# Seven products in place of eight for the down projection of a linear-attention and dense-experts kernel

## The chip, the cores and the metric

The kernel runs on one core of a Trainium2 chip. The metric is the device time of one execution in microseconds (us), as a median over runs. A core has engines with queues of their own: TensorE (PE in the profile; its weight loads are shown apart as PEld), VectorE (DVE), ScalarE (ACT), GpSimd (POOL) and SyncE (SP), which issues the DMAs here. Each engine works through its own instructions in the order in which the program issues them, and waits on semaphores for the others.

## The reference

Eight batches of 512 tokens with 128 channels, all in float32. First linear attention with a normalisation ahead, then a sum over eight experts.

```python
def _L0_attn_ref(x, gamma, beta, w_qkv, w_out, b_out):
    xn = (x - mean) / jnp.sqrt(var + EPS) * gamma + beta
    q, k, v = jnp.split(jnp.einsum('bnc,ck->bnk', xn, w_qkv), 3, axis=2)
    ...
    k = jax.nn.softmax(k, axis=1)
    context = jnp.einsum('bnhd,bnhe->bhde', k, v)
    out = jnp.einsum('bhde,bnhd->bnhe', context, q)
    ...
    return jnp.einsum('bnk,kc->bnc', out, w_out) + b_out + x

def _L0_ffn_ref(hidden_states, Wg, Wu, Wd):
    x = hidden_states.reshape(-1, H)
    def expert_step(acc, w):
        wg, wu, wd = w
        h = jax.nn.silu(x @ wg) * (x @ wu)
        return (acc + h @ wd, None)
    ...

x = x + _layernorm(_L0_attn_ref(_layernorm(x), ...))
x = x + _layernorm(_L0_ffn_ref(_layernorm(x), Wg, Wu, Wd))
```

Wg and Wu are 8 x 128 x 512, Wd is 8 x 512 x 128: with blocks of 128 there are 8 x 4 = 32 blocks of h for each token.

## The kernel before

**The main loop** (from line 564 on) runs over units: batches 0 and 7 are cut into two halves of 256 tokens each, batches 1 to 6 are whole, so there are ten units. For each unit it takes 32 steps (NSTEP: 8 experts times NF = 4 blocks of 128 hidden channels). A step i is:

- g = wg' zT (line 572) and u = wu' zT (574) on TensorE, each a product of a 128x128 block of weights with zT, the normalised batch with channels in partitions and 512 (or 256) tokens side by side, each into one of two PSUM buffers;
- sg = silu(g) on ScalarE (576), h = sg * u on VectorE (578);
- the down product of the step LAG = 2 earlier (line 532, function down): acc += wd' h, 32 such products in one PSUM bank;
- one turn of `others`, which is between(n): it gives every generator that is going one turn, in other words the work of one segment up to the next `yield`.

A float32 product shows as two records of the matmul and two of the weight load.

**Beside the steps** run two generators. attention(b + 1) makes the next batch's zT, and so counts its way in steps: pair_stats of x; the scaling to xh; the move to channels (to_channels); the activation to xnT; k, its maximum and its exponential; x1 and the bias; the move to tokens (to_tokens); the product g_ps, then c, m and wa, one step each; and after_wa, which forms y, normalises it, adds the residual (x2, on GpSimd), normalises again (z) and moves z to channels, which gives zT. finish(b) normalises the finished sum of the unit before, adds x2 on GpSimd and stores the result.

**Moves.** For batches 2 and later a change between tokens and channels in partitions goes in two parts: VectorE transposes blocks of 32x32 (lines 224 and 233), then carry() writes the tile to a DRAM buffer ("bounce", line 215) and reads it back in four DMAs (line 217), all on SP's queue. After it the generator yields LANDING = 4 times. Batches 0 and 1 transpose on TensorE in place of it.

**Normalisations.** norm_stats and pair_stats take statistics on VectorE and then one power on GpSimd (lines 172 and 194: rstd); norm_apply scales in four pieces on VectorE (line 200), which waits for that power.

**Order.** Nothing is reordered: what an engine does next is what the program issued next. In the loop a step issues g, u, sg, h, then the down product of an earlier step, then the segment of the generators. So the segment of step i stands on VectorE behind h of step i and ahead of h of step i + 1.

Of the kernel before, what the change touches and what calls it, by code (L numbers as in the profile page):

```python
# [1 line left out]

# [8 lines left out]
ALU = mybir.AluOpType  # L11
# [4 lines left out]
def kernel(  # L16
# [31 lines left out]


    nc = tc.nc  # L50
    B, N, C = x.shape
# [5 lines left out]
    NQ = P // Q  # L57
    LANDING = 4
    BY_TENSORE = (0, 1)
# [7 lines left out]
    xp = ctx.enter_context(tc.tile_pool(name="xp", bufs=3))  # L67
    work = ctx.enter_context(tc.tile_pool(name="work", bufs=2))
    small = ctx.enter_context(tc.tile_pool(name="small", bufs=3))
    hp = ctx.enter_context(tc.tile_pool(name="hp", bufs=4))  # L70
    dram = ctx.enter_context(tc.tile_pool(name="dram", bufs=4, space=bass.MemoryType.DRAM))
    blk = ctx.enter_context(tc.tile_pool(name="blk", bufs=2))
    ps_gu = ctx.enter_context(tc.tile_pool(name="ps_gu", bufs=2, space=bass.MemoryType.PSUM))
    ps_acc = ctx.enter_context(tc.tile_pool(name="ps_acc", bufs=1, space=bass.MemoryType.PSUM))
    ps = ctx.enter_context(tc.tile_pool(name="ps", bufs=3, space=bass.MemoryType.PSUM))

# [73 lines left out]
    def keep_warm(moving, count=1):  # L150

        t = ps_acc.tile([P, N], F32, tag="acc", name="unread")
        for i in range(count):
            nc.tensor.matmul(
                t[:, : moving.shape[1]], moving[:, :P], moving,
                start=(i == 0), stop=(i == count - 1),
            )


    def norm_stats(src, name):  # L160

        n = src.shape[1]
        stats = small.tile([P, n, 6], F32, tag=f"stats{n}", name=f"stats_{name}")
        mv = small.tile([P, n, 2], F32, tag=f"mv{n}", name=f"mv_{name}")
        for j in range(n):
            nc.vector.bn_stats(stats[:, j, :], src[:, j])
        for j in range(n):
            nc.vector.bn_aggr(mv[:, j, :], stats[:, j, :])  # L168
        ve = small.tile([P, n], F32, tag=f"ve{n}", name=f"ve_{name}")
        nc.vector.tensor_scalar_add(ve, mv[:, :, 1], EPS)  # L170
        rstd = small.tile([P, n], F32, tag=f"rstd{n}", name=f"rstd_{name}")
        nc.gpsimd.tensor_tensor(rstd, ve, mhalf[:, :n], ALU.pow)  # L172
        return mv, rstd
# [23 lines left out]
    def norm_apply(dst, src, mv_rstd):  # L197
        mv, rstd = mv_rstd
        for j in range(src.shape[1]):
            nc.vector.tensor_scalar(  # L200
                dst[:, j], src[:, j], mv[:, j, 0:1], rstd[:, j : j + 1],
                ALU.subtract, ALU.mult,
            )
# [32 lines left out]
    def by_block(t, n=NJ):  # L236

        return t.rearrange("c (j a i) -> c a j i", j=n, a=NQ)

    def flat(t):  # L240
        return t.rearrange("p j c -> p (j c)")
# [6 lines left out]
    def opening():  # L248
# [14 lines left out]
        ek = flat(work.tile([P, NQ, P], F32, tag="ek", name="ek_0"))  # L263
        v = const.tile([P, N], F32, name="v_0")
        qT = const.tile([P, N], F32, name="qT_0")
        x1 = work.tile([P, NJ, C], F32, tag="x1", name="x1_0")
        x1b = work.tile([P, NJ, C], F32, tag="x1b", name="x1b_0")
        x2 = xp.tile([P, NJ, C], F32, tag="x2", name="x2_0")
        x2s[0] = x2
        y = work.tile([P, NJ, C], F32, tag="y", name="y_0")  # L270
        yn = work.tile([P, NJ, C], F32, tag="yn", name="yn_0")
        z = work.tile([P, NJ, C], F32, tag="z", name="z_0")
        zT = work.tile([P, NQ, NJ, Q], F32, tag="zT", name="zT_0")
        kmax = small.tile([P, 3], F32, tag="kmax0", name="kmax_0")
# [101 lines left out]
    def attention(b):  # L376
        xt = xs[b]
        mv, r1, r2 = pair_stats(xt, f"1_{b}")
        yield
        xh = work.tile([P, NJ, C], F32, tag="xh", name=f"xh_{b}")  # L380
        norm_apply(xh, xt, (mv, r2))
# [6 lines left out]
        else:  # L388
            xhT = work.tile([P, NQ, P], F32, tag="xhT", name=f"xhT_{b}")
            to_channels(xh, xhT, f"xh_blk_{b}")  # L390
# [18 lines left out]
        nc.vector.reciprocal(rsum, ksum)  # L409
        x1b = work.tile([P, NJ, C], F32, tag="x1b", name=f"x1b_{b}")  # L410
        for j in range(NJ):
# [44 lines left out]
        y = work.tile([P, NJ, C], F32, tag="y", name=f"y_{b}")  # L456
        yn = work.tile([P, NJ, C], F32, tag="yn", name=f"yn_{b}")
        z = work.tile([P, NJ, C], F32, tag="z", name=f"z_{b}")
        zT = work.tile([P, NQ, NJ, Q], F32, tag="zT", name=f"zT_{b}")
        lags = [after_wa(b, lo, hi, xt, xnT, wa, x1b, x2, y, yn, z, zT) for lo, hi in WHOLE]  # L460
# [7 lines left out]
    def after_wa(b, lo, hi, xt, xnT, wa, x1b, x2, y, yn, z, zT):  # L468
# [11 lines left out]
        s3 = norm_stats(y[:, r], f"3_{b}_{lo}")  # L480
        yield
        norm_apply(yn[:, r], y[:, r], s3)
        (nc.gpsimd if b or lo else nc.vector).tensor_tensor(  # L483
# [4 lines left out]
        s4 = norm_stats(x2[:, r], f"4_{b}_{lo}")  # L488
        yield
        norm_apply(z[:, r], x2[:, r], s4)  # L490
        yield
# [9 lines left out]

    def finish(b, lo, hi, f):
        r = slice(lo, hi)
        n = hi - lo
        if n < NJ:
            f_ps = transpose4(f, f"f_ps_{b}_{lo}")
            f3 = f_ps.rearrange("p (j b k) -> p j b k", j=NJ, b=NQ)[:, :n]
        else:
            for _ in range(LANDING if b + 2 < B else 2 * LANDING):
                yield  # L510
            f3 = f.rearrange("p b (j k) -> p j b k", j=NJ)
        s5 = norm_stats(f3, f"5_{b}_{lo}")
        yield
        fn = work.tile([P, NJ, C], F32, tag="fn", name=f"fn_{b}_{lo}")
        norm_apply(fn[:, :n].rearrange("p j (b k) -> p j b k", b=NQ), f3, s5)
        o = work.tile([P, NJ, C], F32, tag="o", name=f"o_{b}_{lo}")
        nc.gpsimd.tensor_tensor(flat(o[:, :n]), flat(fn[:, :n]), flat(x2s[b][:, r]), ALU.add)  # L517
        nc.sync.dma_start(out[b].rearrange("(p j) c -> p j c", j=NJ)[:, r], o[:, :n])

    units = [(b, lo, hi) for b in range(B) for lo, hi in parts(b)]  # L520
    NSTEP = E * NF
    LAG = 2
    accs, fTs, hs = {}, {}, {}
    pending = []

    def down(n, i):
        b, lo, hi = units[n]
        if i == 0:
            accs[n] = ps_acc.tile([P, N], F32, tag="acc", name=f"acc_{n}")
        e, f = divmod(i, NF)  # L530
        cols = (hi - lo) * P
        nc.tensor.matmul(  # L532
            accs[n][:, :cols], wd_sb[e][:, f, :], hs.pop((n, i)),
            start=(i == 0), stop=(i == NSTEP - 1),
        )
        if i == NSTEP - 1:
            acc = accs.pop(n)[:, :cols].rearrange("c (a j i) -> c a j i", a=NQ, j=hi - lo)
            if hi - lo < NJ:
                fT = work.tile([P, N], F32, tag="fT", name=f"fT_{n}")
                nc.vector.tensor_copy(by_block(fT[:, :cols], hi - lo), acc)  # L540
                fTs[n] = fT[:, :cols]
            else:
                fTs[n] = work.tile([P, NQ, P], F32, tag="f", name=f"f_{n}")
                to_tokens(acc, fTs[n], f"f_blk_{n}")

    def between(n):

        b, lo, hi = units[n]
        if lo == 0 and b + 2 < B:
            xs[b + 2] = load_x(b + 2)  # L550
        going = rest[:]
        rest.clear()
        if n == 0:
            going.append(prepare())
        if hi == NJ and b + 1 < B:
            going.append(attention(b + 1))
        for i in range(NSTEP):
            if i == LAG + 1 and n > 0:
                going.append(finish(*units[n - 1], fTs.pop(n - 1)))
            going = [g for g in going if next(g, "end") != "end"]  # L560
            yield

    opening()
    for n, (b, lo, hi) in enumerate(units):
        zT = zTs.pop((b, lo))
        cols = (hi - lo) * P
        others = between(n)
        for i in range(NSTEP):
# [5 lines left out]
            nc.tensor.matmul(u_ps[:, :cols], wu_sb[e][:, w], zT, start=True, stop=True)  # L574
            sg = hp.tile([P, N], F32, tag="sg", name=f"sg_{n}_{i}")
            nc.scalar.activation(sg[:, :cols], g_ps[:, :cols], AF.Silu)  # L576
            h = hp.tile([P, N], F32, tag="h", name=f"h_{n}_{i}")
            nc.vector.tensor_tensor(h[:, :cols], sg[:, :cols], u_ps[:, :cols], ALU.mult)  # L578
            hs[n, i] = h[:, :cols]
            pending.append((n, i))  # L580
            if len(pending) > LAG:
                down(*pending.pop(0))
            next(others, None)
        for _ in others:
            pass
    while pending:
        down(*pending.pop(0))
    for _ in finish(*units[-1], fTs.pop(len(units) - 1)):
        pass
# [31 lines left out]
```

## Time and profile before

| | us |
|---|---|
| median of 3 runs (721.27 to 721.45) | 721.32 |
| the profiled execution | 721.76 |
| its span, first to last instruction | 719.8 |
| unit 0, first half of batch 0 | 41.8 |
| unit 1, second half of batch 0 | 49.6 |
| unit 2, batch 1 | 85.1 |
| units 3 to 7, batches 2 to 6, each | 85.7 |
| unit 8, first half of batch 7 | 42.5 |

A unit is counted from its first g to the next unit's first g. The rest of the span is the opening of 22.7 us (the attention of batch 0, with the first weights on their way) and the last unit with its end.

How to read the lines: a line of the timeline has the start and the length in us, the engine, the line of the kernel, the operation, what it writes and reads, its shape, how many instructions are merged in it, and in brackets the engine's idle time before it and what ended that. A line of the groups has the busy time of all its instructions, the mean of one in ns, and the idle time before them. Matmuls are pipelined: the time from one start to the next is what one costs, not the length of its record. PEclk is the clock granted to TensorE, as a share of full speed.

### The profile page before, as it was taken

To read this page: it belongs to the slowest core of one execution; us is meant where nothing else is said; L and a number is where in the kernel's file an instruction comes from. 1 tells how busy PE (TensorE), PEld (TensorE's weight loads), DVE (VectorE), ACT (ScalarE), POOL (GpSimd) and SP (SyncE) were. 2 spreads that over 40 slices of the span, in tenths; PEclk is the share of its full clock that TensorE was granted. 3 is DMA by queue.
4 is the path that set the end of the run, shared out by engine and by line. 5 is a ranking of instruction groups with operands and counts; after the bars stand their busy time and mean duration, and the time that the engine had idled before them with its cause. 6 is when DMAs were issued, how large, how long until landed. Compare 5 with 4: busy or idle time off the path is not lost. (4 is left out here: it accounts for less than half of the span.)

```text
span 719.8 us, 6734 instructions
## 1 busy us (share of the span) xinstructions
PE 705.7 (98%) x2177; PEld 397.7 (55%) x2177; DVE 311.7 (43%) x872; ACT 200.9 (28%) x378; POOL 75.5 (10%) x101
## 2 busy tenths in 40 slices
PE   7899999999999999999999999999999999999996
PEld 5788786444444544445444444444444454488885
DVE  4534545435345352444444444443534535243433
ACT  3323332422224122241223322242222412222221
POOL 3100111101002010020100110010100201000000
PEclk9999999999999999999999999999999999999999
DMA  8400000010110001110101101010001100000000
GB/s 268 145 1 0 23 1 15 22 31 0 44 60 34 11 15 29 59 45 0 45 8 51 45 0 44 30 45 30 0 29 47 42 15 12 18 31 15 8 1 8
DMA packets 27299, 23.83 MB, mean 33 GB/s; under 512 B 2944, under 2 KB 20480, under 8 KB 27264
## 3 DMA queue, kind: packets, MB, share of 16 engines
q1 hardware_dynamic: 27120, 23.28, 10.0%
q8 instruction: 17, 0.28, 0.2%
q14 instruction: 18, 0.15, 0.1%
q10 hardware_dynamic: 144, 0.13, 0.1%
HBM read 15.01 MB, written 8.39 MB: 33 GB/s over the span
## 5 line engine op out<-in xcount | busy, mean ns | idle before, releaser
L578 DVE TENSOR_TENSOR h<-sg,u 128x512 f32<-128x512 f32 (+1 forms) x320 | 185.4, 581 | 357.4 <-PE u L574 339.3
L576 ACT ACTIVATE sg<-g 128x512 f32<-128x512 f32 (+1 forms) x320 | 163.5, 511 | 481.8 <-PE g L572 445.1
L572 PE MATMUL g<-zT,wg 128*128 128x512 f32 (+1 forms) x640 | 272.6, 507 | 0.7 <-ACT zT L495 0.5
L574 PE MATMUL u<-zT,wu 128*128 128x512 f32 (+1 forms) x640 | 272.3, 507 | 0.0
L532 PE MATMUL acc<-h,wd 128*128 128x512 f32 (+1 forms) x640 | 272.1, 507 | 0.1
L532 PEld LDWEIGHTS acc<-h,wd 128*128 128x128 f32 x640 | 121.4, 190 | 99.3 <-issue 91.8
L574 PEld LDWEIGHTS u<-zT,wu 128*128 128x128 f32 x640 | 121.3, 190 | 98.9 <-issue 86.3
L572 PEld LDWEIGHTS g<-zT,wg 128*128 128x128 f32 x640 | 118.3, 190 | 84.5 <-issue 77.0
L172 POOL TENSOR_TENSOR rstd<-ve,mhalf 128x4 f32<-128x4 f32 (+1 forms) x28 | 25.9, 926 | 394.3 <-DVE ve L170 394.2
L194 POOL TENSOR_TENSOR rstd<-ve,mhalf 128x8 f32<-128x8 f32 x7 | 11.5, 1637 | 185.6 <-DVE ve L187 185.6
L412 POOL TENSOR_TENSOR x1b<-x,bias_sb 128x128 f32<-128x128 f32 x28 | 12.1, 462 | 23.1 <-DVE x L200 23.1
L517 POOL TENSOR_TENSOR o<-fn,x 128x512 f32<-128x512 f32 (+1 forms) x10 | 10.5, 1050 | 20.7 <-DVE fn L200 18.9
L200 DVE TENSOR_SCALAR x<-x,mv,rstd 128x128 f32<-128x128 f32 x32 | 11.1, 406 | 0.1
L483 POOL TENSOR_TENSOR x<-yn,x 128x512 f32<-128x512 f32 (+1 forms) x8 | 9.6, 1201 | 11.8 <-DVE yn L200 10.5
L200 DVE TENSOR_SCALAR xh<-x,mv,rstd 128x128 f32<-128x128 f32 x32 | 8.8, 336 | 2.1 <-POOL rstd L194 1.8
L429 PEld LDWEIGHTS g_ps<-ek,xh 128*128 128x128 f32 x56 | 7.3, 191 | 4.5 <-issue 2.9
L168 DVE BATCH_NORM_AGGREGATE mv<-stats 128x2 f32<-128x6 f32 x96 | 9.6, 157 | 0.0
L200 DVE TENSOR_SCALAR z<-x,mv,rstd 128x128 f32<-128x128 f32 x32 | 9.0, 341 | 1.3 <-POOL rstd L172 1.3
L200 DVE TENSOR_SCALAR yn<-y,mv,rstd 128x128 f32<-128x128 f32 x32 | 9.0, 341 | 1.3 <-POOL rstd L172 1.3
L476 DVE TENSOR_TENSOR y<-y_ps,x1b 128x512 f32<-128x512 f32 (+1 forms) x9 | 5.7, 632 | 8.2 <-PE y_ps L472 8.2
L404 ACT ACT_TABLE_LOAD x7 | 9.0, 1283 | 0.1
L576 ACT ACT_TABLE_LOAD x7 | 9.0, 1283 | 0.1
(115 smaller groups left out, 199.9 us busy)
## 6 DMA issues: line engine op xcount, KB each, us to landing
wg<-in_L_ffn_Wg_dram SPq DMA_DIRECT2D x8, 256.0 KB, 6.0
wu<-in_L_ffn_Wu_dram SPq DMA_DIRECT2D x8, 256.0 KB, 5.9
wd<-in_L_ffn_Wd_dram SPq DMA_DIRECT2D x8, 256.0 KB, 6.1
x<-in_L_attn_x_dram SPq DMA_DIRECT2D x7, 256.0 KB, 2.8
bounce<-xh_blk SPq DMA_DIRECT2D x6, 256.0 KB, 2.0
xhT<-bounce SPq DMA_DIRECT2D x24, 64.0 KB, 2.0
bounce<-ek_blk SPq DMA_DIRECT2D x6, 256.0 KB, 2.0
ek<-bounce SPq DMA_DIRECT2D x24, 64.0 KB, 2.0
```

The costliest lines, as they stand in the source:

```text
L168: nc.vector.bn_aggr(mv[:, j, :], stats[:, j, :])
L172: nc.gpsimd.tensor_tensor(rstd, ve, mhalf[:, :n], ALU.pow)
L194: nc.gpsimd.tensor_tensor(rstd, ve, mhalf, ALU.pow)
L200: nc.vector.tensor_scalar(dst[:, j], src[:, j], mv[:, j, 0:1], rstd[:, j : j + 1], ALU.subtract, ALU.mult,)
L412: nc.gpsimd.tensor_tensor(x1b[:, j, :], x1[:, j, :], bias_sb, ALU.add)
L483: (nc.gpsimd if b or lo else nc.vector).tensor_tensor(flat(x2[:, r]), flat(yn[:, r]), flat(xt[:, r]), ALU.add)
L517: nc.gpsimd.tensor_tensor(flat(o[:, :n]), flat(fn[:, :n]), flat(x2s[b][:, r]), ALU.add)
L532: nc.tensor.matmul(accs[n][:, :cols], wd_sb[e][:, f, :], hs.pop((n, i)), start=(i == 0), stop=(i == NSTEP - 1),)
L572: nc.tensor.matmul(g_ps[:, :cols], wg_sb[e][:, w], zT, start=True, stop=True)
L574: nc.tensor.matmul(u_ps[:, :cols], wu_sb[e][:, w], zT, start=True, stop=True)
L576: nc.scalar.activation(sg[:, :cols], g_ps[:, :cols], AF.Silu)
L578: nc.vector.tensor_tensor(h[:, :cols], sg[:, :cols], u_ps[:, :cols], ALU.mult)
```

## The change

Whole batches take the down projection in another way; the halves keep the old one (down()).

**Pairs.** Two successive blocks of h (k = 0 and 1), each 128 hidden channels by 512 tokens, cut into left and right 256 tokens, and the two blocks of wd, cut into 64 low and 64 high output channels, are two 2x2 matrices of blocks. Their product is formed by seven block products (a form of Strassen's algorithm) in place of eight. Each block product has 128 hidden channels, 64 output channels, and 256 tokens.

- Four sums of blocks of the weights are made once for each pair by weight_sums() on GpSimd (32 operations of 128 elements for each partition), as a generator during unit 0.
- Four sums of blocks of h, t2, are made for each pair by three subtractions on GpSimd (one of 512 and two of 256 elements for each partition) behind the odd step.
- down_pairs() issues the products, 16 steps (8 pairs, GROUP = 16) at a time, LAG steps after the last of them: 56 products in a row, in turn one whose output lies in PSUM partitions 0 to 63 (below) and one in 64 to 127 (above). Two PSUM banks, A and D, take the sums of the seven products; the product p4 goes to D and A by turns, so that each half has the same number.
- finish_pairs() transposes and carries both banks (two carries in place of one), yields LANDING times, joins the partial sums with seven additions on VectorE, and goes on to last_norm(), the former end of finish().

**Waiting times in steps.** LANDING is 5 in place of 4; attention() yields once more after pair_stats; after_wa() yields once more before each scaling of a whole batch; last_norm() does so too. The finish of a unit starts when its down products have been issued.

**Memory.** The pool `work` has one buffer in place of two for each tile; x1b shares x1, yn shares y, xhT shares ek, o shares fn; zT and sg have pools of their own; h2 and t2 have nine buffers each. The PSUM pool ps has two buffers in place of three, and the bank set free is D.

```diff
-    LANDING = 4
+    LANDING = 5
...
-    work = ctx.enter_context(tc.tile_pool(name="work", bufs=2))
+    work = ctx.enter_context(tc.tile_pool(name="work", bufs=1))
+    zp = ctx.enter_context(tc.tile_pool(name="zp", bufs=2))
...
+    pairp = ctx.enter_context(tc.tile_pool(name="pairp", bufs=9))
...
-    ps = ctx.enter_context(tc.tile_pool(name="ps", bufs=3, space=bass.MemoryType.PSUM))
+    ps = ctx.enter_context(tc.tile_pool(name="ps", bufs=2, space=bass.MemoryType.PSUM))
...
@@ attention
         mv, r1, r2 = pair_stats(xt, f"1_{b}")
         yield
+        yield
         xh = work.tile([P, NJ, C], F32, tag="xh", name=f"xh_{b}")
...
@@ after_wa
         s3 = norm_stats(y[:, r], f"3_{b}_{lo}")
         yield
+        if hi - lo == NJ:
+            yield
...
         s4 = norm_stats(x2[:, r], f"4_{b}_{lo}")
         yield
+        if hi - lo == NJ:
+            yield
...
+    def finish_pairs(b, lo, hi, sums):
+        f = []
+        for name, acc in zip("AB", sums):
+            t = work.tile([P, NQ, P], F32, tag=f"blk{name}", name=f"f_blk{name}_{b}")
+            nc.vector.transpose(
+                t.rearrange("p a (s j k) -> p a s j k", s=2, j=2),
+                acc.rearrange("c (s a j i) -> c a s j i", s=2, a=NQ, j=2),
+            )
+            f.append(work.tile([P, NQ, P], F32, tag=f"f{name}", name=f"f{name}_{b}"))
+            carry(f[-1], t)
+            yield
+        for _ in range(LANDING if b + 2 < B else 2 * LANDING):
+            yield
...
+        nc.vector.tensor_tensor(u, p1, p6, ALU.add)
+        nc.vector.tensor_tensor(c11, p1, p2, ALU.add)
+        nc.vector.tensor_tensor(p4, p4, p4b, ALU.add)
+        yield
+        nc.vector.tensor_tensor(c21, u, p7, ALU.add)
+        nc.vector.tensor_tensor(c12, u, p5, ALU.add)
+        nc.vector.tensor_tensor(c22, c21, p5, ALU.add)
+        both = q[:, 2:6].rearrange("p (s b) x -> p s b x", s=2)
+        nc.vector.tensor_tensor(both, both, D[:, 0], ALU.add)
+        yield
...
+        yield from last_norm(b, lo, hi, f3)
+
+    def last_norm(b, lo, hi, f3):
+        n = hi - lo
         s5 = norm_stats(f3, f"5_{b}_{lo}")
         yield
+        if n == NJ:
+            yield
...
+    GROUP = 16
...
+    def weight_sums():
+        for e in range(E):
+            w = wd_sb[e].rearrange("p (q k) c -> p q k c", k=2)
+            a11, a21, a12, a22 = (w[:, :, k, c : c + HALF] for k in (0, 1) for c in (0, HALF))
+            t = ws_sb[e]
+            for i, (a, b, op) in enumerate((
+                (a21, a22, ALU.add), (t[:, :, 0], a11, ALU.subtract), (a11, a21, ALU.subtract),
+                (a12, t[:, :, 1], ALU.subtract),
+            )):
+                nc.gpsimd.tensor_tensor(t[:, :, i], a, b, op)
+                if i % 2:
+                    yield
...
+    def down_pairs(n, g, pairs):
...
+        for two in range(0, len(pairs), 2):
+            below, above = [], []
+            for m, (h, t) in enumerate(pairs[two : two + 2]):
...
+                below += [
+                    (A[low, left], w0[:, low], h[:, 0], first, False),
+                    (A[low, right], w1[:, low], h[:, 2], False, end),
+                    (D[low, right], sm[:, 3], h[:, 3], first, end),
+                ]
+                above += [
+                    (D[high, right], sm[:, 0], t[:, 0], first, False),
+                    (A[high, right], sm[:, 1], t[:, 2], first, False),
+                    (D[high, left], sm[:, 2], t[:, 1], False, end),
+                ]
+                if m == 0:
+                    below.append((D[low, left], w1[:, high], t[:, 3], False, False))
+                else:
+                    above.append((A[high, left], w1[:, high], t[:, 3], False, end))
+            for two_tiles in zip(below, above):
+                for o, w, r, start, stop in two_tiles:
+                    nc.tensor.matmul(o, w, r, start=start, stop=stop)
+        if (g + 1) * GROUP == NSTEP:
+            fins[n] = finish_pairs(b, lo, hi, accs.pop(n))
...
@@ between
         for i in range(NSTEP):
-            if i == LAG + 1 and n > 0:
-                going.append(finish(*units[n - 1], fTs.pop(n - 1)))
+            if n - 1 in fins:
+                going.append(fins.pop(n - 1))
...
@@ the main loop
-            hs[n, i] = h[:, :cols]
-            pending.append((n, i))
-            if len(pending) > LAG:
-                down(*pending.pop(0))
-            next(others, None)
+            if not whole:
+                due.append((count + LAG, partial(down, n, i, h)))
+            elif i % 2:
+                t2 = pairp.tile([P, 4, N // 2], F32, tag="t2", name=f"t2_{n}_{i}")
+                pairs.append((h2, t2))
+                if len(pairs) == GROUP // 2:
+                    due.append((count + LAG, partial(down_pairs, n, i // GROUP, pairs)))
+                    pairs = []
+            while due and due[0][0] <= count:
+                due.pop(0)[1]()
+            next(others)
+            if whole and i % 2:
+                nc.gpsimd.tensor_tensor(t2[:, 0:2], h2[:, 1::2], h2[:, 0:2], ALU.subtract)
+                nc.gpsimd.tensor_tensor(t2[:, 2], h2[:, 3], t2[:, 0], ALU.subtract)
+                nc.gpsimd.tensor_tensor(t2[:, 3], h2[:, 2], t2[:, 2], ALU.subtract)
+            count += 1
```

## The prediction

> **What bounds the kernel now.** I read the page first: its first part (busy time by engine), then its stretches.
>
> ```profile
> span 719.8 us, 6734 instructions
> PE 705.7 (98%) x2177; PEld 397.7 (55%) x2177; DVE 311.7 (43%) x872; ACT 200.9 (28%) x378; POOL 75.5 (10%) x101
> ```
>
> TensorE is busy 98% of the span. The sums by stretch, for one whole batch (from its first gate product to the next batch's), say whether it ever waits there:
>
> ```profile
> core 0: us, PE busy (x) PEld busy (x) DVE busy (x) ACT busy (x) POOL busy (x), PEclk, DMA share, GB/s
> 199.14:284.85 85.71, 85.71 (x217) 39.32 (x216) 37.68 (x101) 23.15 (x37) 8.95 (x10) 1.00 0.10 31
> ```
>
> It doesn't: 85.71 of 85.71 us, at the full granted clock (1.00). The timeline gives the pitch:
>
> ```profile
> 300.30 1.02 PE L572 MATMUL g<-zT,wg 128*128 128x512 f32 x2
> 301.16 1.02 PE L574 MATMUL u<-zT,wu 128*128 128x512 f32 x2
> 302.02 1.02 PE L532 MATMUL acc<-h,wd 128*128 128x512 f32 x2
> 302.29 0.69 DVE L578 TENSOR_TENSOR h<-sg,u 128x512 f32<-128x512 f32 x1 [1.89 <-PE u L574]
> 302.88 1.02 PE L572 MATMUL g<-zT,wg 128*128 128x512 f32 x2
> ```
>
> Starts lie 0.858 us apart, so a step of three products takes 2.574 us; 32 steps are 82.4, and the rest of the 85.71, 3.3 us, is the next batch's attention. So every TensorE microsecond saved counts, and so does every new wait. The same timeline, around the hand-over to the next batch, shows work that is hidden today:
>
> ```profile
> 265.11 1.02 PE L574 MATMUL u<-zT,wu 128*128 128x512 f32 x2
> 266.84 0.70 DVE L224 STREAM_TRANSPOSE z_blk<-z 128x512 f32<-128x512 f32 x1
> 267.58 0.34 SPq L215 DMA_DIRECT2D bounce<-z_blk  x1
> 269.74 1.73 SPq L217 DMA_DIRECT2D zT<-bounce  x4
> ```
>
> ```profile
> DMA to landing us min/median/max: 1.8/2.0/2.1
> ```
>
> The last line is from the view of tile zT. The transpose starts 1.73 us after its step's up product; the fourth read of the bounce is issued at 269.74 + 1.73 - 0.43 (one issue) = 271.04 and lands 2.0 later, at 273.0. From transpose to landed zT: 6.2 us. Today that is step 24 of 32, seven steps (18 us) early.
>
> **Part 1: the products.** Six whole batches (1 to 6) change; the halves of batches 0 and 7 don't. Before: 32 x 0.858 = 27.46 us for each. After: 16 pairs x 7 products = 112, in 56 rounds of two, each product 64 columns wide and 256 long. Half batches show the pitch of 256 columns:
>
> ```profile
> 650.36 0.59 PE L532 MATMUL acc<-h,wd 128*128 128x256 f32 x2
> 650.79 0.59 PE L572 MATMUL g<-zT,wg 128*128 128x256 f32 x2
> ...
> 23.67 0.30 PEld L140 LDWEIGHTS bv_ps<-beta_sb,w_qkv_sb 128*128 128x128 f32 x2
> ```
>
> One product alone takes 0.43 us. No row has two side by side; a round costs between 0.432 (they overlap wholly) and 0.864 (not at all). The third row bounds the weight loads: two in 0.30 us, the last 0.19 long, so one each 0.11; four in a round are 0.44 at most, so loads alone don't forbid the lower end. I take 0.432, since the row that the round is nearest to is one product of that length, and the two use separate columns and output partitions; 0.864 is a rival. 56 x 0.432 = 24.19: saved 3.27 per batch, 19.6 us in all; the other end costs 56 x 0.432 x 6 = 145 us more.
>
> The Trainium skill, "TensorE: Matmul & The Clock Gate", Part 3, has three 32-column products at once 2.38 times as fast as in turn; by that rate, as an estimate, a round would be nearer 0.54, with 18 us lost where I have 19.6 gained.
>
> **Part 2: entering and leaving a burst.** Twelve bursts (two for each batch). With products in the order low, low, high, high (each float32 product is two records), the first half-slot is not shared: 0.216 us. At each edge the pipe may empty: from nothing to the tail of a record (0.592 mean against 0.429 pitch, 0.16) plus a load (0.19). So 0.2 to 0.9 for a burst; I take 0.6, between, since no row switches: 7.2 us (2.6 to 11).
>
> The skill's "TensorEngine Tiling (Array Packing)", Key Properties, says that a change of tiling mode drains TensorE. No row here shows it; it speaks for the upper end, 11 us.
>
> **Part 3: steps get shorter, and zT comes late.** Outside the bursts a step is now g and u, 1.716 us. attention() counts in steps, and gets five more: one after pair_stats, one for each of the two landings (4 to 5), two in after_wa. Counting its yields, the transpose of z moves from step 24 to step 29. The second burst doesn't cover it: due at count + LAG, it is issued in step 1 of the next batch, behind that batch's first gate product in TensorE's order, and this product needs zT. From up product 29's start: transpose +1.73, zT +7.9; the next batch's g is due at 5 x 0.858 = +4.29. TensorE waits 3.6 us at each hand-over to batches 2 to 7 (batch 1 goes by TensorE): 6 x 3.6 = 21.6 us. Behind the waiting g stand u, the next g and u, and the burst; ScalarE and VectorE then idle. The landing itself is priced from its own rows, so the bounds are narrow.
>
> By the skill's clock page, Part 1, an idle window of about 3.4 us halves the clock. In the whole batches of this trace TensorE never waits and its clock is 1.00, so no row tests it; by the rule each such wait might lose up to 1.7 us more, an estimate.
>
> **Part 4: POOL and VectorE.** Every pair gets three subtractions. The rows:
>
> ```profile
> L517 POOL TENSOR_TENSOR o<-fn,x 128x512 f32<-128x512 f32 x6 | 7.6, 1267 | 15.8 <-DVE fn L200 15.8
> L517 POOL TENSOR_TENSOR o<-fn,x 128x256 f32<-128x256 f32 x4 | 2.9, 724 | 4.9 <-DVE fn L200 3.1 <-POOL rstd L172 1.8
> 178.55 1.11 DVE L200 TENSOR_SCALAR z<-x,mv,rstd 128x128 f32<-128x128 f32 x4
> 227.42 1.41 DVE L200 TENSOR_SCALAR x<-x,mv,rstd 128x128 f32<-128x128 f32 x4
> 227.84 1.74 POOL L412 TENSOR_TENSOR x1b<-x,bias_sb 128x128 f32<-128x128 f32 x4 [1.41 <-DVE x L200]
> ```
>
> 1.27 + 2 x 0.72 = 2.71 us for a pair, 43 for a batch, beside today's 9: 52 of some 88, so POOL keeps up; its last subtraction has the 10 us of the burst to land. weight_sums adds 32 POOL operations of 128 elements (x1b: 0.46) = 15 us under batch 0's first half (41.8 us; POOL busy 1.4 there), after the last wd has landed or just behind it: nothing.
>
> But POOL is busy 2.71 of each 3.43 us, and the last three rows show what that does: four scalings alone take 1.11 us, beside POOL's adds 1.41, their later pitch 0.40 in place of 0.26. A scaling held until one of the longer subtractions ends costs more. z's scaling (step 28) starts amid the odd step's subtractions: 0 to 0.9 us later, straight onto the zT wait; I take half: 6 x 0.45 = 2.7 (0 to 5.4).
>
> The product h has 2.57 us from the end of its u to the start of the u that reuses the bank, and needs 0.27 + 0.69: a slack of 1.6 us, where today's 4.29 leave 3.3. In it now come finish_pairs' two transposes (0.71 each; two carries, so ten SP issues in place of five, ahead of xh's carry, due five steps later: covered), seven additions (0.3 to 0.43 each) and the statistics. Around step 10 ScalarE's switch to Exp and back holds sg: from k_ps's end (223.17) to sg's end (226.78) are 3.61 us, against 2 x 1.716 = 3.43 available: 0.2 to 0.25 late. The additions in step 9, four beside POOL's, are 0 to 1.2 late. I take 0.75 per batch: 4.5 us (1.5 to 9).
>
> **Sum**, against the profiled execution's own time, 721.76 (span 719.8 and 1.96 around it): -19.6 + 7.2 + 21.6 + 2.7 + 4.5 = +16.4, 738.2. The median of the runs, 721.32, is 0.44 lower: 738. The case's own bounds: +6.1 gives 727, +27.4 gives 749. The tail of batch 7 and the opening are untouched.
>
> **Rivals.**
>
> *zT lands in time* (faster). Were there no hand-over wait, 738 - 24.3 = 714; with the bounds of parts 2 and 4, 705 to 720. For it: only zT stands between u 31 and the next g, and a count of yields can be off. Against: today's transposes sit where the count puts them. It decides once the wait falls below (19.6 - 7.2 - 4.5) / 6 = 1.3 us.
>
> *The tiles share only part of the time.* If a load can't pass the other half's waiting product, a round is 0.432 + two exposed loads of 0.055 (64 columns, half of 0.11) = 0.544, or 0.654 with full loads: 336 rounds x 0.112 or 0.222 = +38 or +75: 776 or 812. For it: in every row the next load begins as a matmul begins. Against: there each load needs the buffer which that start frees; the halves have their own.
>
> *The tiles don't overlap*, so that the change saves no TensorE time: +145, 883. For it: no matmul here shares the array. Against: two one-column products (L140) start 0.03 us apart, so a new one may enter while the last drains.
>
> **Chances.** Forecast 57%, zT in time 18%, partly shared 13%, not shared 12%. The time is the forecast's, 738 (its own range 727 to 749). The range 706 to 790 leaves out the unshared case, half of the 812 and the edge of the fast case, under 2 in 10. About 0.2% (1.4 us) is what a measurement of this kernel tells from no change: faster 0.17 (the zT rival), within 0.04 (the seam between it and the forecast), slower 0.79.
>
> **What would show it.** Part 1: twelve bursts of 12.1 us; 15 or 24 refute it. Part 2: the gap of TensorE at each burst's edges. Part 3: the first g of batches 2 to 7 released by the landing of zT, after 3.6 to 4.5 us of idle. Part 4: three subtractions of 2.7 us per pair, scalings of over 0.5 us, and waits of u for h around steps 9 to 12. I am wrong if the g's wait is short or if a burst is not near 12 us.

## The result and the profile after

The changed kernel takes 781.32 us (median of 4 runs, 780.28 to 781.67) against 721.38 for the kernel before in the same comparison: a ratio of 1.0825, interval 1.0809 to 1.0842. It is slower, as forecast, by 60 us rather than 16. The profiled execution took 781.67 with a span of 779.8. The first part of its page, and the last rows of its stretches:

```profile
span 779.8 us, 9053 instructions
PE 710.2 (91%) x3137; PEld 422.4 (54%) x3137; DVE 359.1 (46%) x920; ACT 200.3 (26%) x378; POOL 349.4 (45%) x421
...
PEclk9999999999899999999899998999989999899999
```

TensorE now idles 70 us of the span (14 before), GpSimd works 349 us in place of 76, and the granted clock dips at each of the six hand-overs to batches 2 to 7 (five show as the 8s of PEclk; the dip at 288.58 us lies across two slices). A whole unit has grown from 85.7 to 95.9 us. Unit 2 has one burst of products less (79.9) and unit 8 one more (54.9), since the second burst of a batch falls into the next unit. Sums by stretch: unit 4, then three stretches at the hand-over to unit 3.

```profile
core 0: us, PE busy (x) PEld busy (x) DVE busy (x) ACT busy (x) POOL busy (x), PEclk, DMA share, GB/s
290.69:386.57 95.88, 86.89 (x376) 43.37 (x377) 45.94 (x108) 23.04 (x37) 52.40 (x58) 0.96 0.10 33
189.27:193.01 3.74, 0.04 (x1) 0.00 (x0) 0.73 (x2) 0.00 (x0) 3.50 (x5) 1.00 0.35 116
193.01:199.84 6.83, 5.45 (x7) 2.38 (x8) 1.59 (x8) 0.60 (x1) 0.81 (x2) 0.50 0.16 52
199.84:212.00 12.16, 12.16 (x109) 7.66 (x109) 1.18 (x6) 0.60 (x1) 4.32 (x4) 1.00 0.00 1
```

The second row is most of the wait, which ends at 194.39; the third is a stretch of 6.83 us at a granted clock of 0.50, of which TensorE works 5.45. The last row holds nearly one whole burst, at full clock. The timeline there, from the transpose of z to the burst's first rounds:

```profile
188.05 0.70 DVE L236 STREAM_TRANSPOSE z_blk<-z 128x512 f32<-128x512 f32 x1
188.77 0.34 SPq L227 DMA_DIRECT2D bounce<-z_blk  x1
190.84 1.73 SPq L229 DMA_DIRECT2D zT<-bounce  x4
194.39 2.05 PE L690 MATMUL g<-zT,wg 128*128 128x512 f32 x2 [5.09 <-DMA zT<-bounce]
...
200.69 0.43 PE L653 MATMUL accA<-h,wd 128*64 128x256 f32 x1
...
200.70 0.43 PE L653 MATMUL accB<-t,ws 128*64 128x256 f32 x1
...
200.96 0.38 PE L653 MATMUL accA<-h,wd 128*64 128x256 f32 x1
...
200.97 0.38 PE L653 MATMUL accB<-t,ws 128*64 128x256 f32 x1
```

The first g of the unit waited 5.09 us for zT, and its two records take 2.05 us, where 1.02 is the rule. In the burst, a record for the upper half starts 3 to 8 ns behind one for the lower half: the two run side by side from the first record on. All twelve bursts last 12.1 us. (In these lines, products that read h are of the lower half, those that read t and ws of the upper.)

Two further waits appear inside the unit. The timeline again (steps 9 to 12; brackets: idle time before, and what ended it):

```profile
228.25 1.36 DVE L552 TENSOR_TENSOR q<-q,fB 128x128 f32<-128x128 f32 x1
...
234.66 1.13 PE L690 MATMUL g<-zT,wg 128*128 128x512 f32 x2 [1.62 <-ACT sg L694]
...
237.35 1.27 POOL L715 TENSOR_TENSOR t<-h 128x512 f32<-128x512 f32 x1
...
237.86 2.70 DVE L213 TENSOR_SCALAR fn<-q,mv,rstd 128x128 f32<-128x128 f32 x4
...
241.22 1.13 PE L692 MATMUL u<-zT,wu 128*128 128x512 f32 x2 [1.87 <-DVE h L701]
```

Four scalings of fn, 1.1 us when alone, take 2.70, beside GpSimd's subtractions (t); the product h stands behind them on VectorE, and u waits 1.87 us for h. One addition (128 elements for each partition, 0.28 us where GpSimd is idle) takes 1.36. The groups of these scalings, before and then after (the last columns: busy us, mean ns of one, idle before; the 25.1 us for zT are five of the six hand-overs, the sixth goes to a half):

```profile
L200 DVE TENSOR_SCALAR z<-x,mv,rstd 128x128 f32<-128x128 f32 x32 | 9.0, 341 | 1.3 <-POOL rstd L172 1.3
L200 DVE TENSOR_SCALAR fn<-f,mv,rstd 128x128 f32<-128x128 f32 x24 | 6.7, 341 | 0.9 <-POOL rstd L172 0.9
```

```profile
L690 PE MATMUL g<-zT,wg 128*128 128x512 f32 x384 | 204.9, 616 | 32.3 <-DMA zT<-bounce 25.1 <-ACT sg L694 7.1
...
L692 PE MATMUL u<-zT,wu 128*128 128x512 f32 x384 | 202.6, 610 | 14.0 <-DVE h L701 14.0
...
L213 DVE TENSOR_SCALAR z<-x,mv,rstd 128x128 f32<-128x128 f32 x32 | 21.6, 732 | 3.2 <-POOL rstd L185 3.2
...
L213 DVE TENSOR_SCALAR fn<-q,mv,rstd 128x128 f32<-128x128 f32 x24 | 14.6, 669 | 0.0
```

The account of unit 4, from gaps between TensorE's starts beyond the usual pitch, against the 85.7 us of a unit before:

| | us |
|---|---|
| products (two bursts for 32 products) | -3.3 |
| edges of the two bursts (0.52 in place of 0.43 going in, 0.31 in place of 0.22 coming out, and their like) | +0.5 |
| next unit's first g waits for zT | +5.1 |
| half clock behind that wait: (288.58 + 6.83 - 290.69) / 2 | +2.4 |
| u waits for h (0.92 behind z's scaling, 2.03 behind fn's) | +3.0 |
| g waits for sg (1.07), k for xnT (0.70) | +1.8 |
| seven gaps of 0.10 us, each between the two records of one product behind a wait or a burst | +0.7 |
| sum, measured | +10.2 |

Six times 10.2 is 61; the profiled executions differ by 59.9. The half-clock stretches of the six hand-overs start at 193.01, 288.58, 384.15, 479.73, 575.30 and 670.87. TensorE is in them for 5.44, 4.72, 4.40, 4.04, 3.98 and 3.72 us, half of which is lost: 13.2 us in all.

### The profile page after: what moved, and what is told of

It reads as the page before. It is cut to its first block, busy times and chain, and to the rows that moved or that the text cites. A ratio compares the mean times of both kernels' runs of the same rounds, so it can differ in the third digit from the quotient of the medians.

```text
span 779.8 us, 9053 instructions
## 1 busy us (share of the span) xinstructions
PE 710.2 (91%) x3137; PEld 422.4 (54%) x3137; DVE 359.1 (46%) x920; ACT 200.3 (26%) x378; POOL 349.4 (45%) x421
## 5 line engine op out<-in xcount | busy, mean ns | idle before, releaser
L690 PE MATMUL g<-zT,wg 128*128 128x512 f32 (+1 forms) x640 | 282.5, 524 | 38.2 <-DMA zT<-bounce 30.4
L715 POOL TENSOR_TENSOR t<-h 128x512 f32<-128x512 f32 x96 | 121.7, 1268 | 161.2 <-DVE h L701 161.0
L653 PE MATMUL accB<-t,ws 128*64 128x256 f32 x384 | 107.0, 381 | 0.0
L653 PE MATMUL accA<-h,wd 128*64 128x256 f32 x384 | 99.2, 381 | 0.0
L604 PE MATMUL acc<-h,wd 128*128 128x256 f32 x256 | 75.9, 379 | 0.0
L717 POOL TENSOR_TENSOR t<-h,t 128x256 f32<-128x256 f32 x96 | 70.7, 736 | 7.5
L716 POOL TENSOR_TENSOR t<-h,t 128x256 f32<-128x256 f32 x96 | 70.4, 733 | 7.5
L653 PEld LDWEIGHTS accA<-h,wd 128*64 128x64 f32 x384 | 51.7, 137 | 35.0 <-PE g L690 4.5
L653 PE MATMUL accA<-t,ws 128*64 128x256 f32 x192 | 57.1, 379 | 0.0
L653 PE MATMUL accB<-h,ws 128*64 128x256 f32 x192 | 57.1, 379 | 0.0
L604 PEld LDWEIGHTS acc<-h,wd 128*128 128x128 f32 x256 | 48.5, 190 | 7.6 <-issue 1.0
L653 PEld LDWEIGHTS accB<-t,ws 128*64 128x64 f32 x384 | 51.7, 137 | 0.0
```

What stands on the lines that cost most here:

```text
L604: nc.tensor.matmul(accs[n][:, :cols], wd_sb[e][:, f, :], h, start=(i == 0), stop=(i == NSTEP - 1))
L653: nc.tensor.matmul(o, w, r, start=start, stop=stop)
L690: nc.tensor.matmul(g_ps[:, :cols], wg_sb[e][:, w], zT, start=True, stop=True)
L715: nc.gpsimd.tensor_tensor(t2[:, 0:2], h2[:, 1::2], h2[:, 0:2], ALU.subtract)
L716: nc.gpsimd.tensor_tensor(t2[:, 2], h2[:, 3], t2[:, 0], ALU.subtract)
L717: nc.gpsimd.tensor_tensor(t2[:, 3], h2[:, 2], t2[:, 2], ALU.subtract)
```

## The experiments

The theory that came out of the trace: a batch pays for three things, the hand-over wait for zT, the halved clock behind it, and VectorE work that GpSimd's subtractions hold up. The rivals were the products themselves (their two halves share less than they seem to) and the steps which the change adds.

**The second burst ahead of the next batch's first g.** After a whole unit's 32 steps, its last burst is issued before anything of the next unit:

```diff
         for _ in others:
             pass
+        if whole:
+            due.pop(0)[1]()
```

> The second burst of a whole batch is issued right after its step 31, ahead of the next batch's first gate product, and so lies under the landing of zT. Theory (the hand-over is the larger part of the loss): in the changed kernel each of six hand-overs costs 5.2 us of TensorE idle and 3.0 us of half-speed records behind it; both go, 6 x 8.2 = 49 us, about 732. Rival (the late zT is only one of several things that are late, and the burst itself then waits for the last pairs' h and t): the idle time moves to the head of the burst, 765 or more. The waits of u for h and of g for sg inside the batches stay in both (about 4.7 us per batch).

731.83 us, ratio 1.0139 (1.0124 to 1.0154): 49.5 us less than the changed kernel, 6 x 8.2. The 12 us of the burst cover zT, and with the wait its half clock is gone. Sums by stretch, unit 4:

```profile
288.24:375.79 87.55, 84.45 (x378) 42.49 (x377) 45.20 (x108) 23.04 (x37) 52.16 (x58) 1.00 0.11 37
```

95.88 has become 87.55, at a clock of 1.00; of these 8.3 us, 5.1 + 2.4 are the wait and the clock, the rest is u's wait for h, which falls from 3.0 to 2.5, and g's for sg (from 1.07 to 0.77). That the expected 8.2 came out is in part luck: the clock was counted at 3.0, and the other two waits were to stay. So a change of the order of issue alone removes zT's lateness, with all five added steps in place. The unit is still 1.8 us above that of before: the waits of u, g and k (3.9 us in unit 4) take back more than the 3.3 us which the products save.

**The clock alone.** Twelve unread products of 256 columns, in place of the idle time ahead of the first g of batches 2 to 7, so that TensorE waits without being idle:

```diff
+        if b >= 2 and lo == 0:
+            fill = ps.tile([P, N], F32, tag="ps", name=f"fill_{n}")
+            for k in range(12):
+                nc.tensor.matmul(fill[:, : N // 2], warm[:, :P], warm, ...)
```

> Twelve products of 256 columns whose result nobody reads (12 x 0.43 = 5.2 us) stand in front of the first gate product of batches 2 to 7, so that TensorE works while it waits for zT. Theory (idleness halves the clock, and that is a cost of its own, 3.0 us at each hand-over): the wait is only filled, but the records behind it run at full pitch, 6 x 3.0 = 18 us less, about 763, granted clock near 1.00 in these slices. Rival (the half-speed records come from something else, such as the landing DMA or the reload of weights): no change, 781, or slower by what the filling overshoots.

774.19 us, ratio 1.0737 (1.0719 to 1.0755): 7.1 less than the changed kernel by the medians, 9.3 by the spans of the profiled executions (this one is the fastest of the four, at a mean clock of 0.993; the others have 0.987 to 0.990). All six stretches of half clock at the hand-overs are gone; two new ones have come. Sums by stretch: behind one hand-over, then inside a unit.

```profile
287.85:294.68 6.83, 6.83 (x39) 3.59 (x40) 2.69 (x12) 1.19 (x2) 2.56 (x2) 1.00 0.08 29
329.60:333.04 3.44, 1.56 (x5) 0.61 (x4) 2.89 (x5) 0.60 (x1) 2.94 (x4) 1.00 0.37 122
333.04:336.45 3.41, 3.41 (x6) 1.35 (x5) 0.69 (x1) 0.60 (x1) 3.25 (x4) 0.50 0.29 102
```

In the second row TensorE is busy for 1.56 of 3.44 us, waiting for h, and the 3.41 us after it run at 0.50. The 18 us of the expectation had counted seven slow records at each hand-over; the overlaps listed above give 13.2, and two new stretches give back 2 x 1.7. That leaves 9.8, against 9.3 measured. So the halved clock is a cost of its own, of about 13 us. The Trainium skill, "TensorE: Matmul & The Clock Gate", Part 1, says that an idle window of about 3.4 us halves the clock; the rows agree, with 0.50 behind idle times of 4.9 to 5.2 us. They also show it behind a 3.44-us stretch in which TensorE was idle for only 1.9, and lasting 6.83 us in place of 3.41 behind the longer waits.

**Without GpSimd's subtractions.** This kernel leaves out the three subtractions of each pair; the products read h in their place, and everything else stands:

```diff
-                pairs.append((h2, t2))
+                pairs.append((h2, h2))
...
-                nc.gpsimd.tensor_tensor(t2[:, 0:2], h2[:, 1::2], h2[:, 0:2], ALU.subtract)
...
```

> Leaves out GpSimd's three subtractions for each pair; the products read h where they read t. Theory (GpSimd's long operations hold VectorE's operations with two inputs in SBUF, and its scalings): the scalings go from 0.54 to 0.73 us back to 0.34, the waits of u for h (3.0 us per batch) go, those of g for sg shrink, and z comes about 1.6 us earlier at each hand-over, because h of step 29 is no longer held up: 6 x (3.0 + 1 + 1.6) = 34 us less, about 747. Rival (VectorE's own added transposes and additions make it late): the waits of u for h stay, at most 10 us less, 771 or more.

747.07 us, ratio 1.036 (1.0342 to 1.0379): 34 us less. The groups:

```profile
L690 PE MATMUL g<-zT,wg 128*128 128x512 f32 x384 | 203.2, 611 | 18.4 <-DMA zT<-bounce 18.0
L692 PE MATMUL u<-zT,wu 128*128 128x512 f32 x384 | 201.0, 605 | 1.2 <-DVE h L701 1.2
...
L213 DVE TENSOR_SCALAR z<-x,mv,rstd 128x128 f32<-128x128 f32 x32 | 9.4, 354 | 0.5 <-POOL rstd L185 0.5
...
L213 DVE TENSOR_SCALAR fn<-q,mv,rstd 128x128 f32<-128x128 f32 x24 | 6.5, 328 | 0.0
```

The scalings are back at 354 and 328 ns (732 and 669 above), u's wait for h falls from 14.0 to 1.2 us, and zT's wait to 3.6 or 3.7 us for each batch (18.0 for five of the six), which is the prediction's count of 3.6 without any delay on VectorE. In unit 4 the waits of u, g and k fall from 4.7 to 0.6 us, though VectorE still has the added transposes and additions. The half clock is still there at five of the six hand-overs; the wait of 3.61 us ahead of batch 2 has none behind it. GpSimd's subtractions cost 34 us, though GpSimd is idle for more than half of the time.

**The products in another order.** Seven products of the lower half, then seven of the upper, in place of one and one:

```diff
-            for two_tiles in zip(below, above):
+            for two_tiles in (below, above):
```

> As the changed kernel, but of each fourteen products the seven of the low half of the array come first and then the seven of the high half, in place of by turns. Theory (products in different halves run side by side only if they stand next to each other in TensorE's order): only the two places where the halves meet are shared, half a product each: 14 x 0.432 - 2 x 0.216 = 5.6 us in place of 3.02, 48 times: +124 us, about 905; bursts of 22.5 us. Rival (TensorE reaches far enough ahead to find them, 64 instructions or so): no change, 781.

860.4 us, ratio 1.1923 (1.1899 to 1.1947), between the two expectations. Bursts take 18.4 us, neither 12.1 nor the 24.2 of products that share nothing. The timeline at a border, from the seven lower products (here those that read h) to the seven upper ones (here t and ws):

```profile
322.40 0.43 PE L653 MATMUL accB<-t,ws 128*64 128x256 f32 x1
322.61 0.38 PE L653 MATMUL accA<-h,wd 128*64 128x256 f32 x1
322.67 0.38 PE L653 MATMUL accB<-t,ws 128*64 128x256 f32 x1
322.82 0.38 PE L653 MATMUL accB<-h,ws 128*64 128x256 f32 x1
322.88 0.38 PE L653 MATMUL accA<-t,ws 128*64 128x256 f32 x1
```

Each half goes on at its own pitch of 0.21 us, 0.06 apart from the other; some way from the border only one half works. TensorE takes a few products of the other half ahead of their turn, not seven: the upper record at 322.40 starts before the last lower product at 322.82, which the program issues first. So "Nothing is reordered", as said of the kernel before, does not hold between the halves. They share the time wholly in the order that the change uses: its bursts of 12.1 us leave no room for the rival of a shared part (15).

**The five added steps.** All but the finish's landing set back to their counts of before:

```diff
@@ attention
         yield
-        yield
...
-            for _ in range(LANDING):
+            for _ in range(LANDING - 1):
...
@@ after_wa (twice)
-        if hi - lo == NJ:
-            yield
```

> As the changed kernel, but attention() and after_wa() have their old number of steps (the landing of the finished sum keeps 5), so that z is transposed in step 24. Theory (the hand-over's 8.2 us come from the five steps alone): they go, 6 x 8.2 = 49 us, less what the earlier segments now wait for (powers behind GpSimd's subtractions, landings of xhT and ek after 6.9 us in place of 8.6): 732 to 745. Rival (the second burst, or the load of zT itself, makes the hand-over late wherever z stands): 775 or more.

800.51 us, ratio 1.1093 (1.1071 to 1.1115): slower, where a gain was expected. The view of waits, TensorE's largest:

```profile
PE u L687 <- DVE h L696: 39.3, 22, 2.9
...
PE k_ps L411 <- ACT xnT L405: 16.8, 6, 3.3
...
PE g_ps L441 <- DMA ek<-bounce: 6.4, 6, 1.6
```

No wait for zT is left, as expected; but waits for h (7.7 us in unit 4, counted from start to start as in the account above; the view counts only the idle time), for xnT (3.3) and for ek (1.1) have come, with half clocks behind the longest. At steps of 1.716 us the powers on GpSimd (z's scaling waits 1.86 us for one) and the landings need the added turns. The theory that the five steps merely cost time falls: they pay for themselves, and the place of the second burst was the thing to change.

**Getting VectorE free.** Each of the next is the first experiment plus one thing. Scalings of whole batches on ScalarE:

```diff
+                nc.scalar.activation(
+                    d, s, AF.Identity, bias=shift[:, j : j + 1], scale=rstd[:, j : j + 1])
```

> On top of e1_burst_ahead, the scalings of whole batches go from VectorE (four operations with mean and rstd) to ScalarE (four activations with scale rstd and bias -mean * rstd, which one more small VectorE operation makes). Theory (the waits of u for h come from scalings that GpSimd's subtractions hold up): these 3.0 us per batch go, 6 x 3.0 = 18 us below e1_burst_ahead, about 714; the waits for sg (1.1 to 1.8) stay or grow by under 0.5. Rival (ScalarE's four activations, 1.2 us or more in front of sg, hold sg as long as h was held before): no less than e1_burst_ahead, 732 or more.

748.95 us, ratio 1.0372 (1.0356 to 1.0387); the rival held. u no longer waits for h, but g waits 6.0 us in each batch for sg, since groups of four scalings of 0.4 stand ahead of it on ScalarE; three stretches of half clock (3.41 us each) come with that.

A form of the scaling that also writes its sum, on VectorE. In this form the shift isn't added, so the mean isn't subtracted in whole batches:

```diff
-                d, s, mv[:, j, 0:1], rstd[:, j : j + 1], ALU.subtract, ALU.mult
+                d, s, rstd[:, j : j + 1], shift[:, j : j + 1], ALU.mult, ALU.add,
+                accum_out=sums[:, j : j + 1],
```

> On top of e1_burst_ahead, VectorE's scalings of whole batches also write out the sum of their result (x * rstd + shift, with shift = -mean * rstd from one more small operation; nobody reads the sums). The Trainium skill, SBUF, Who interferes with whom, says that the form of tensor_scalar that writes its accumulator does not enter the two-port mode in which VectorE and GpSimd exclude each other. Theory (the scalings are late because GpSimd's subtractions hold a port that they want): a scaling takes 0.3 to 0.4 us beside the subtractions too, the waits of u for h (2.7 us per batch) fall below 0.5, 6 x 2.3 = 14 us below e1_burst_ahead, about 718. Rival (they are held by something that both forms share, such as the order of the queue or the memory itself): scalings of 0.5 to 0.7 us, 731 or more.

727.33 us, ratio 1.0081 (1.0065 to 1.0098), 4.5 less than the first experiment. The groups:

```profile
L223 DVE TENSOR_SCALAR_CACHE_REDUCE z<-x,rstd,shift 128x128 f32<-128x128 f32 x28 | 9.7, 402 | 0.3
L223 DVE TENSOR_SCALAR_CACHE_REDUCE fn<-q,rstd,shift 128x128 f32<-128x128 f32 x24 | 8.3, 402 | 0.2
L559 DVE TENSOR_TENSOR q<-fA 128x128 f32<-128x128 f32 x6 | 7.0, 1173 | 0.0
```

The scalings are a flat 402 ns with the subtractions going on (they start 0.33 us apart, the plain ones alone 0.26), so that this form isn't held; the additions, which read two tiles, still are (1173). The Trainium skill, "SBUF — State Buffer", section "Who interferes with whom", says just this: the plain scaling can, and an operation with two SBUF inputs does, contend with GpSimd for a shared pair of ports; the form that writes out its accumulator doesn't. With the scalings free, u still waits 1.97 us for h, because the scalings of x1 and of fn fall into one step. The hold by GpSimd is one part of the matter, the crowd in one step another.

The same with the seven additions on GpSimd, one more step for them, and xh's landing one step longer:

```diff
-        nc.vector.tensor_tensor(u, p1, p6, ALU.add)
+        nc.gpsimd.tensor_tensor(u, p1, p6, ALU.add)
...
```

> On top of e5_scales_with_sum, the seven additions of finish_pairs go from VectorE to GpSimd, with one more step behind them, and the landing of xhT gets one more step. Theory: VectorE then has no operation left that wants GpSimd's port, the maximum ahead of the exponential is no longer late (0.8 us per batch), nor k's product behind xhT (0.7): 6 x 1.5 = 9 us less, about 709. Rival (GpSimd's queue is now so full that the power of the statistics and t come late): 718 or more.

734.19 us (728.72 to 736.37), ratio 1.0163 (1.012 to 1.0205): a miss. An addition takes 455 ns on GpSimd, and u's wait for h (1.99) and g's for sg (1.53) are no shorter than before. The trace is that of the fastest execution, 728.72, at a mean clock of 0.999; the other three have 0.988 to 0.992, so that part of their 733 to 736 us is likely a halved clock, which this trace doesn't show.

**Spreading the work.** Back on the first experiment, with the real scalings: z's and fn's scaling cut into two turns each, fn three steps later, xh's landing one step longer and ek's one shorter.

```diff
+            norm_apply(z[:, r], x2[:, r], s4, (0, 1))
+            yield
+            norm_apply(z[:, r], x2[:, r], s4, (2, 3))
```

> On top of e1_burst_ahead, the steps are set anew and nothing else: the scalings of z and of the finished sum are cut into two turns of two operations each, the latter three steps later, so that it no longer meets the scaling of x1 in one step; the landing of xhT gets one more step and that of ek one less. Theory (what is left over the best case in e1_burst_ahead is work that falls into one step: u behind the scalings 2.7 us per batch, k behind xhT 0.7, g behind the exponential's late maximum 0.5 of 0.8): 6 x 3.5 = 21 us less, about 711, faster than the kernel before (721.4). Rival (GpSimd's subtractions hold VectorE wherever its work stands): at best a third of it, 725 or more.

719.93 us, ratio 0.998 (0.9971 to 0.9989): between theory and rival, and 0.2% less than the kernel before. Then x1's scaling in two turns as well, ek's landing one step shorter again, and the second group of additions in two turns:

```diff
+        norm_apply(x1, xt, (mv, r1), (0, 1))
+        yield
+        norm_apply(x1, xt, (mv, r1), (2, 3))
...
-            for _ in range(LANDING - 1):
+            for _ in range(LANDING - 2):
```

> On top of e9_spread_out, the scaling of x1 is cut into two turns as well (the landing of ek gives up one more step), and the second group of finish_pairs' additions into two. Theory: in e9_spread_out u waits 1.4 us per batch for h, 1.1 of it behind the scaling of x1 and 0.2 behind the additions; 6 x 1.3 = 8 us less, about 712. Rival (the wait only moves to the step that now has more): no less than 718.

717.7 us, ratio 0.9943 (0.9929 to 0.9956): the fastest, 0.6% less than the kernel before. Most of the wait only moved, as the rival had it: in unit 4 u's wait for h falls from 1.37 to 0.24 us, and g's for sg rises from 0.46 to 1.42. Then the statistics of the finished sum five turns later, behind the exponential:

```diff
+        for _ in range(5):
+            yield
         yield from last_norm(b, lo, hi, f3)
```

> e10 with the last norm's statistics five turns later, so that they don't stand ahead of the exponential's maximum on VectorE. If g's wait for sg (1.42 us per batch in e10) comes from that order, it falls to about 0.25: 1.2 x 6 = 7 us less than e10's 717.7, about 711. Rival: the work moved later meets the next step's scalings and the wait only changes its name: 716 or more.

718.47 us, ratio 0.9961 (0.9947 to 0.9975): the rival held. From the view of waits, TensorE's longest in the kernel just before (717.7), then in this one:

```profile
PE g L706 <- ACT sg L710: 7.0, 6, 1.3
```

```profile
PE u L710 <- DVE h L719: 4.8, 10, 0.8
```

g's wait for sg (1.42 us for each batch) is down to 0.23, as expected, and u's wait for h is up from 0.24 to 1.51, most of it at y's scaling, which is held for 3.15 us there. Cutting that one in two needs a turn that isn't there (the attention already ends with the unit's last step), and wasn't tried. Sums by stretch, unit 4 of the fastest kernel:

```profile
284.41:369.40 84.99, 83.65 (x379) 42.70 (x377) 47.54 (x108) 23.13 (x37) 52.36 (x58) 1.00 0.12 38
```

84.99 us: of the 3.3 us that the products save, 0.7 are left.

## Why the prediction was right and wrong

The direction was right, and so were the products and the place of the hand-over's wait. Two steps failed: "I take 0.75 per batch" in Part 4, where 4.7 us came, and the sum's silence on the halved clock, which cost 13.2 us. The forecast's sum was +16.4, the profiled execution shows +59.9. That 781 still lies between 706 and 790 is luck: the range reached so far for the rival of partly shared products (776), not for what happened; the forecast's own bounds ended at 749.

- **Part 1, the products: right.** A round takes 0.431 us (0.432 forecast), a burst 12.1. That rules out both rivals that priced less sharing (15 and 24 us); the order experiment shows what less sharing costs.
- **Part 2, the edges: too dear.** 0.6 for each burst was forecast, about 0.25 measured: 3 us in place of 7.2 (with the small gap behind each burst, 4). That "the first half-slot is not shared" was wrong, the halves start 3 to 8 ns apart. The drain that the Trainium skill, "TensorEngine Tiling (Array Packing)", Key Properties, tells of may be in the 0.1 us at each side, and is no more than that here.
- **Part 3, the hand-over: its term was too small, by a cost that the sum left out.** The wait was named at the right place, with its releaser; "3.6 us" is 3.7 without the subtractions and 4.9 to 5.2 with them (forecast 4.05 with Part 4's delay): 30.4 us in all, against 24.3. But the halved clock stood in a sentence by itself and counted nothing: 13.2 us. "So the bounds are narrow" was the failed step here. It bounded the landing, but neither the clock of the products behind an idle TensorE, since no row of the kernel before had such a wait, nor a z that comes later than Part 4 has it.
- **Part 4, "I take 0.75 per batch": the largest miss.** u's waits for h, g's for sg and k's for xnT are 4.7 us for each batch: 28 us where 4.5 stood. The prediction had the rows (scalings at 0.40 in place of 0.26 beside GpSimd) and wrote that a longer subtraction costs more, but then allowed z's group of four scalings a delay of 0 to 0.9 us in all, and none to the groups of fn and x1 in the 0.75. The changed kernel's timeline at z's scaling:

```profile
280.74 1.26 POOL L715 TENSOR_TENSOR t<-h 128x512 f32<-128x512 f32 x1
280.80 3.15 DVE L213 TENSOR_SCALAR z<-x,mv,rstd 128x128 f32<-128x128 f32 x4 [0.46 <-POOL rstd L185]
282.08 0.72 POOL L716 TENSOR_TENSOR t<-h,t 128x256 f32<-128x256 f32 x1
282.88 0.72 POOL L717 TENSOR_TENSOR t<-h,t 128x256 f32<-128x256 f32 x1
```

The four scalings take 1.29, 0.88, 0.88 and 0.33 us. Each of the first three ends 0.08 us after one of the three subtractions, the fourth stands beside none: a scaling is held anew by each subtraction, and the group takes 3.15 us in place of 1.11. What the prediction looked for around steps 9 and 10 was right in part: without the subtractions g's wait for sg is 0.23 us, as it had it (0.2 to 0.25). The experiment without subtractions confirms the size: 34 us in all, zT's and the clock's share included.
- **Rivals.** zT in time was wrong for this kernel, but what it would be worth was underestimated: with the second burst moved ahead, 49.5 us come back (30.4 of the wait, 13.2 of the clock, the rest of u's and g's waits), not 24.3, and the result (731.83) is still slower than before because of Part 4.

Of the difference of 43.5 us, then, about 24 are VectorE's lateness, 13 the clock, 6 a longer zT wait, 4 to 5 small gaps, less 4 at the edges. What stays open is why a first product's records stand 0.10 us further apart (the small gaps, 0.7 us in each unit).

## What to carry to other kernels

Before shortening TensorE's work in a loop at 98% of it, count for each other engine what it must do within the shorter step: here the steps went from 2.57 to 1.72 us, and TensorE, which had waited for nothing inside a whole batch, waited 4.7 us in each for h, sg and xnT. When work moves to GpSimd, price every VectorE scaling and every addition of two tiles beside it as one that may be held, one by one and not once for a group. And a burst that needs nothing of the next stage belongs ahead of that stage's first instruction in the queue: these two lines were worth 49.5 us.

## What the hardware showed that I had not expected

The stretches of half clock start 95.57 us apart, which is 28 times 3.413, though the waits that bring them are 95.6 to 96.3 apart: they fall on a fixed grid, so that much the same wait loses 2.7 us in one batch and 1.9 in another. Two records for different halves of the columns start 3 to 8 ns apart and run at the pitch of one. When the halves come in groups of seven, TensorE still finds about two products to share at each border ((24.2 - 18.4) / 7 borders = 0.8 us, at 0.43 each). And the scaling that also writes a sum costs 399 to 407 ns with or without subtractions beside it, where the plain one takes from 332 to 1286.
